# Two head groups to a tile in layer 0's attention, side work one step earlier in attentions 1 and 3, folding in other PSUM banks, and the last rows of two expert blocks in both halves of the array's rows

## The chip, the cores and the metric

The kernel runs on one core of a Trainium2 chip. The metric is the device time of one execution in microseconds. A core has five engines that work beside each other: TensorE (PE in the profile: matrix products into PSUM, with its weight loads shown as PEld), VectorE (DVE), ScalarE (ACT), GpSimd (POOL) and SyncE (SP, which here only issues transfers).

## What is computed

The reference is a network of four layers on x of shape (4, 256, 256), that is four batches of 256 tokens with 256 features, all in float32. Each layer adds an attention over a context (4, 512, 128) and then a feed-forward part:

```python
x = x + L0_xattn(layernorm(x), ctx, ...)   # 16 heads of 16; the last 16 context rows have a softmax of their own,
                                           # ctx @ Wo + bo with both results added
x = x + L0_ffn(layernorm(x), ...)          # 64 arrows of rank 16, the 4 longest of each token
x = x + L1_xattn(layernorm(x), ctx, ...)   # 16 heads of 128 on 8 key/value heads
x = x + L1_ffn(layernorm(x), ...)          # 8 experts of 176, 2 of each token, and a shared expert of 352
x = x + L2_xattn(...);  x = x + L2_ffn(...)  # two experts of 512, one of each token
x = x + L3_xattn(...);  x = x + L3_ffn(...)  # the 64 strongest tokens of each batch through 256-1024-256
```

An expert of layer 1 computes `silu(x @ wg.T) * (x @ wu.T) @ wd.T`. Its 176 inner features are 128 + 48, so its down product is one matmul with 128 contraction rows and one with 48.

## The kernel before

**Order.** The body stands in `tc.manual_schedule`, with the engines PE, ACT, DVE and POOL in the order in which the program is written: each engine takes its instructions strictly in that order, so where a call stands decides what waits behind what. Loads are issued on SP's queue. The stages are, in microseconds of the profiled span: layer 0's attention 0 to 153, its FFN with the folding of layer 1's weights to 243, attention 1 to 576, layer 1's FFN with folding of layer 2 to 702, attention 2 to 1035, layer 2's FFN with folding of layer 3 to 1091, attention 3 to 1436, and the last FFN.

**PSUM.** Up to the end of layer 0's FFN, `bank` (L850) hands out a ring of six banks for all tags but "o", which has two. Later there are four banks "s", two "mm", one "t" and one "o". A tile in a bank waits until the previous tile in it has been read.

**Layer 0's attention.** The loop at L1585 goes over batches b and four head groups hg of four heads, each in two steps (kp), so that a batch has steps i = 0 to 7. A step computes the scores of four heads (L1321: heads of 16 rows in the four 32-row groups of the array), their exponentials on ACT (L1325), and the products with the values of the step before (L1331, L1340). The value tile has 32 columns for a head: 16 columns of ones, which give the sums, and 16 of values. So a head group's result has 128 rows, half of which are sums. `quotient` (L1348) transposes within blocks of 32, takes reciprocals, transposes back and multiplies, all on DVE; POOL adds the two softmaxes into `oT[:, hg]` (L1360). `output0` (L1362) multiplies the four head groups' tiles with `wo0`, whose rows for the sums' places are zero, in four accumulating matmuls for each chunk of 128 tokens. `output_bias` (L1278) does it once for the bias. `ahead` works for the next batch: projections, and at i = 2 to 4 the norm of keys and queries, whose last step is the product at L1231 on DVE into `pad`; that is transposed at L1296 at the head of steps 6 and 7. `between` calls `output0(b - 1)` at i = 4 and 5:

```python
            if b > 0 and i in (4, 5):
                output0(b - 1, (i - 4,))
```

**Layer 0's FFN** goes over eight chunks with class `Arrows` (L1384); `turned` (L1435) transposes what POOL made in `twof` (L1427), `output` makes the result.

**Folding.** `folding` (L974) joins query and key weights into `m_sb` (L985 on PE, L993 on ACT) and value and output weights into `n_sb` (L1001 on PE, L1004 on DVE), eight times two heads for a layer, as a generator whose steps the stages take in between their own work.

**Layer 1's FFN.** `chosen` and `turned1` make the routing as side work of attention 1: `beside1` (L2117) is called at each unit hp of a batch. The pairs of token and expert are sorted into 23 blocks of 128 slots (NBLK), each of one expert, whose number is read into a register. A block gathers its tokens, transposes them (`turn_in`, L2303, one bank "t"), copies its expert's gate and up weights (`weights`, L2317 on DVE), makes gate and up (`rise`, L2325), silu on ACT and product on DVE, and then in `fall` the down products (L2341 with 128 rows, L2344 with 48), scaled by ACT (L2348) and stored by SP. The loop keeps three blocks going:

```python
                    blocks[j + 2].weights()
                    blocks[j + 2].turn_in()
                if 0 <= j + 1 < NBLK:
                    blocks[j + 1].rise()
                if 0 <= j < NBLK:
                    blocks[j].fall()
```

**Layers 2 and 3.** `Block2.turn_in` (L2605) does the same for layer 2's blocks. `beside3` (L3051) has the last layer's routing (class `Router`) as side work of attention 3.

Of the kernel before, what the change touches and what calls it, by code (L numbers as in the profile page):

```python
# [9 lines left out]
F32 = mybir.dt.float32  # L10
# [3 lines left out]
ALU = mybir.AluOpType  # L14
# [821 lines left out]
def bounded_path(ctx: ExitStack, tc: tile.TileContext, t, out: bass.AP, over):  # L836
# [137 lines left out]
    def folding(L, m_sb, n_sb):  # L974

        for i in range(4):
# [4 lines left out]
            for g in range(2):  # L981
# [18 lines left out]
                pn = bank("mm", [P, 2, D], f"pn_{L}_{i}_{g}")  # L1000
# [25 lines left out]
    with tc.manual_schedule(engines={E.PE, E.Activation, E.DVE, E.Pool}):  # L1026
# [42 lines left out]
        wo0 = l0.tile([P, 4, D], F32, tag="wo0", name="wo0")  # L1069
        nc.sync.dma_start(wo0, t["L0_wo"].rearrange("(g p) n -> p g n", p=P))  # L1070
# [34 lines left out]
        vals = [l0.tile([P, NK, H0, 32], F32, tag=f"vals{i}", name=f"vals{i}") for i in range(2)]  # L1105
        vals_d = [l0.tile([P, H0, 32], F32, tag=f"vals_d{i}", name=f"vals_d{i}") for i in range(2)]

        def ones_of_values():
# [9 lines left out]
            for i in range(2):  # L1118
                nc.gpsimd.memset(vals[i][:, : NK - 1, :, :HD0], 1.0)
                nc.gpsimd.tensor_copy(  # L1120
                    vals[i][:, NK - 1, :, :HD0], rows[:, 0:1, None].to_broadcast([P, H0, HD0])
                )
                nc.gpsimd.tensor_copy(vals_d[i][:, :, :HD0], rows[:, 1:2, None].to_broadcast([P, H0, HD0]))
# [61 lines left out]
        def project_v(b):  # L1185

            wv = by_head(wkv, 2 * HD0)[:, :, :, HD0:]
            for k0 in range(0, NK + 1, 2):
                pv = bank("mm", [P, 2, H0, HD0], f"pv{b}_{k0}")
                for k in range(k0, min(k0 + 2, NK + 1)):  # L1190
                    ck = c_last[:, b % 2, k - NK + 1, :] if k >= NK - 1 else cT[:, b, k * P : (k + 1) * P]
                    nc.tensor.matmul(pv[:, k - k0], lhsT=ck, rhs=wv[:, int(k == NK)], start=True, stop=True)
                if k0 < NK:
                    nc.scalar.copy(vals[b % 2][:, k0 : k0 + 2, :, HD0:], pv)
                else:
                    nc.scalar.copy(vals_d[b % 2][:, :, HD0:], pv[:, 0])
# [67 lines left out]
        bcol = l0.tile([P, 4, P], F32, tag="bcol", name="bcol")  # L1264

        def bias_rows():

            nc.vector.tensor_tensor(brow[:, 0, :], brow[:, 0, :], brow[:, 1, :], ALU.add)

        def bias_columns():  # L1270
            pc = bank("o", [P, 4], "pbrow")
            for g in range(4):
                nc.tensor.matmul(
                    pc[:, g : g + 1], lhsT=brow[:, 0, g * P : (g + 1) * P], rhs=ident[:1, :1], start=True, stop=True
                )
            nc.vector.tensor_copy(bcol, pc[:, :, None].to_broadcast([P, 4, P]))

        def output_bias():  # L1278
            pb = bank("mm", [P, D], "pbo")
            for g in range(4):  # L1280
# [1915 lines left out]
```

## Time and profile before

| what | value |
|---|---|
| median of 3 runs | 1453.56 us (1453.41 to 1455.87) |
| profiled execution, its own time | 1455.58 us |
| its span, first to last instruction | 1453.9 us |
| granted TensorE clock, mean | 0.994 |
| TensorE busy | 1421.4 us, 98% |
| DVE, ACT, POOL busy | 63%, 40%, 47% |
| output0's matmuls (L1366) | 64 records, mean 390 ns |
| down product, 128 rows and 48 rows (L2341, L2344) | 46 records each, mean 383 and 428 ns |

Times in the profile are microseconds from the span's start. A row of a timeline has the start, the duration, the engine, the line, the operation, the tile written and the tiles read, the shape and the number of records. Square brackets name how long the engine had been idle and the instruction that ended it. A float32 matmul leaves two records.

### The profile page before, as it was taken

The numbers are of one execution on the slowest core, as the hardware profiler recorded it, in microseconds if no ns is written. First come the engines' busy times: TensorE is split into PE (matmuls) and PEld (weight loads), VectorE is DVE, ScalarE is ACT, GpSimd is POOL, SyncE is SP. The second block draws the span as 40 slices with busy tenths as digits, with TensorE's granted clock in tenths as the row PEclk, the third lists the DMA queues.
The fourth block names the chain that finished last, engine by engine and source line by source line (L and its number), as shares of the span: only waits on it lengthen the run. The fifth ranks groups of instructions, "written<-read, shape, count | busy, mean of one in ns | idle before, by whom it ended". The sixth has DMA issues, their size and how long they took to land.

```text
span 1453.9 us, 20222 instructions
## 1 busy us (share of the span) xinstructions
PE 1421.4 (98%) x7421; PEld 937.0 (64%) x7421; DVE 914.0 (63%) x2004; ACT 585.9 (40%) x1124; POOL 677.1 (47%) x796
## 2 busy tenths in 40 slices
PE   9999999999999999999999999999999999999998
PEld 7665676566556666777556666655875566666656
DVE  6666773666676556543576666548755766767675
ACT  4666343433433332244543333333454433333331
POOL 2222232576655454131366665665314765456560
PEclk9999999999999999999999999999999999999999
DMA  5000220310000001164020000000331000000000
GB/s 167 2 2 2 73 72 1 79 32 0 8 1 8 1 8 32 39 203 103 30 72 2 23 1 1 8 0 8 95 124 44 19 1 1 0 1 0 0 1 32
DMA packets 49591, 47.06 MB, mean 32 GB/s; under 512 B 8169, under 2 KB 45386, under 8 KB 49484
## 3 DMA queue, kind: packets, MB, share of 16 engines
q1 hardware_dynamic: 45884, 37.56, 8.6%
q0 software_dynamic: 2496, 6.82, 1.8%
q8 instruction: 61, 1.00, 0.3%
q10 hardware_dynamic: 1104, 1.31, 0.3%
q14 instruction: 46, 0.38, 0.1%
HBM read 38.86 MB, written 6.82 MB: 31 GB/s over the span
## 4 chain that ended last, share of the span: by engine, by line
PE 88%; DVE 7%; POOL 2%; issue 1%; ACT 1%; DVEq 0%; ACTq 0%; POOLq 0%
PE ps L1817 22%; PE po L1825 21%; PE paq L1787 5%; PE pao L1787 4%; PE pbq L1787 4%; PE pbo L1787 4%; PE pgu L2325 2%; PE ps L1321 2%; PE pyf L1448 2%; PE po L1331 2%; PE paf L1398 1%; PE py L1907 1%; PE pm L985 1%; PE psh L2161 1%; PE pn L1001 1%
## 5 line engine op out<-in xcount | busy, mean ns | idle before, releaser
L1836 POOL TENSOR_TENSOR half<-pT 128x1024 f32<-128x1024 f32 x93 | 218.8, 2353 | 322.6 <-ACT pT L1820 255.2
L1817 PE MATMUL ps<-qT,cT 128*128 128x512 f32 x768 | 345.5, 592 | 0.0
L1825 PE MATMUL po<-pT,c_sb 128*128 128x512 f32 x768 | 345.3, 592 | 0.0
L1820 ACT ACTIVATE pT<-ps,mbias 128x512 f32<-128x512 f32 x384 | 263.7, 687 | 155.5 <-PE ps L1817 143.9
L1825 PEld LDWEIGHTS po<-pT,c_sb 128*128 128x128 f32 x768 | 145.8, 190 | 183.2 <-issue 183.2
L1817 PEld LDWEIGHTS ps<-qT,cT 128*128 128x128 f32 x768 | 138.9, 190 | 138.4 <-issue 137.0
L1829 ACT COPY oT<-po 128x512 f32<-128x512 f32 x96 | 56.2, 586 | 265.0 <-PE po L1825 265.0
L1872 POOL TENSOR_TENSOR oT<-oT,wide 128x512 f32<-128x512 f32 x90 | 115.5, 1304 | 27.9 <-DVE wide L1871 27.9
L1325 ACT ACTIVATE pT<-ps 128x512 f32<-128x512 f32 x128 | 66.1, 603 | 37.8 <-PE ps L1321 37.6
L1797 DVE TENSOR_TENSOR qT<-qT,paq 128x128 f32<-128x128 f32 x90 | 25.5, 283 | 85.8 <-ACT qT L1796 85.7
L1797 DVE TENSOR_TENSOR w<-w,pao 128x128 f32<-128x128 f32 x21 | 6.0, 285 | 109.4 <-ACT w L1796 109.4
L1844 DVE TENSOR_TENSOR half<-half 128x512 f32<-128x512 f32 x96 | 71.0, 740 | 2.5 <-POOL half L1836 2.2
L1846 DVE STREAM_TRANSPOSE turned<-half 128x512 f32<-128x512 f32 x96 | 68.3, 712 | 6.3
L1787 PEld LDWEIGHTS paq<-xnT_a,m_sb 128*128 128x128 f32 x360 | 57.9, 191 | 21.5 <-issue 10.6
L1787 PE MATMUL paq<-xnT_a,m_sb 128*128 128x128 f32 x360 | 71.4, 280 | 0.1
L1787 PE MATMUL paq<-xx,m_x 128*128 128x128 f32 x360 | 69.8, 276 | 0.0
L1850 DVE TENSOR_REDUCE sums<-turned 128x16 f32<-128x512 f32 x96 | 65.9, 686 | 3.4
L1787 PE MATMUL pao<-n_x,ox 128*128 128x128 f32 x336 | 65.4, 276 | 0.3 <-POOL ox L1713 0.3
L1871 DVE STREAM_TRANSPOSE wide<-rz 128x512 f32<-128x512 f32 x96 | 62.2, 686 | 0.1
L1796 ACT COPY qT<-paq 128x128 f32<-128x128 f32 x90 | 23.9, 265 | 89.9 <-PE paq L1787 89.8
L1800 DVE TENSOR_TENSOR qT<-qT,pbq 128x384 f32<-128x384 f32 x90 | 49.9, 554 | 9.4
L1787 PEld LDWEIGHTS paq<-xx,m_x 128*128 128x128 f32 x360 | 54.6, 192 | 0.0
(445 smaller groups left out, 2612.9 us busy)
## 6 DMA issues: line engine op xcount, KB each, us to landing
wo<-in_L_wo SPq DMA_DIRECT2D x12, 512.0 KB
wq<-in_L_wqT SPq DMA_DIRECT2D x11, 512.0 KB
yd<-yr SPq DMA_DIRECT2D x23, 128.0 KB
w<-in_F_w SPq DMA_DIRECT2D x4, 512.0 KB
xd<-xn_f SPq DMA_DIRECT2D x7, 256.0 KB
wk<-in_L_wkT SPq DMA_DIRECT2D x11, 128.0 KB
wv<-in_L_wvT SPq DMA_DIRECT2D x11, 128.0 KB
x_sb<-in_x SPq DMA_DIRECT2D x4, 256.0 KB
```

The costliest lines, as they stand in the source:

```text
L1325: nc.scalar.activation(pT[kp][:, j], ps[j], AF.Exp)
L1787: nc.tensor.matmul(p[:, at, :], lhsT=lhsT, rhs=rhs, start=(k == 0 and at == 0), stop=(k == len(of) - 1 and i == which[-1]),)
L1817: nc.tensor.matmul(ps, lhsT=cT[:, b, k * P : (k + 1) * P], rhs=qT, start=True, stop=True)
L1820: nc.scalar.activation(pT[:, k, :], ps, AF.Exp, bias=mbias[:, b, k : k + 1])
L1825: nc.tensor.matmul(po, lhsT=c_sb[:, b, k, :], rhs=pT[:, k], start=(k == 0), stop=(k == NK - 1))
L1829: done["head"] = nc.scalar.copy(raw, po).ins
L1836: nc.gpsimd.tensor_tensor(half, pT[:, 0:2], pT[:, 2:4], ALU.add)
L1844: nc.vector.tensor_tensor(part, half[:, 0], half[:, 1], ALU.add)
L1846: nc.vector.transpose(turned.rearrange("p f i -> p (f i)"), part)
L1850: nc.vector.tensor_reduce(sums[b, hp // 4][:, hp % 4, :], turned, AX.X, ALU.add)
L1871: nc.vector.transpose(wide, rzs[b, hp // 4][:, hp % 4, :, None].to_broadcast([P, NB, 32]))
L1872: eng.tensor_tensor(outs[b, hp], outs[b, hp], wide.rearrange("p f i -> p (f i)"), ALU.mult)
```

## The change

1. **Heads of layer 0 packed.** The values of even head groups go to columns 16 to 31 of a head's 32, those of odd ones to columns 0 to 15, with the ones in the other half (`halves`). So an even and an odd group fill opposite halves of one tile of `oT`, into which POOL adds: `oT`, `wo0`, the bias rows and columns have 2 parts instead of 4. The value weights are sorted into `wvo` by four copies on POOL; the reciprocals are put into a tile whose other half is zero, so that the sums' places become zero. `wo0` is loaded in eight transfers of 32 KB in place of one of 512 KB. (The value tiles, the fills with ones and the bias rows are indexed to match; these lines are left out below.)
2. **Layer 0's order.** `output0(b - 1)` stands at i = 6 and 7 for b = 1 and 2; the first `Arrows`' turned and output stand before `output0(B - 1)`.
3. **Folding.** After layer 0 the tile `pn` is in the banks "o" and "t" by turns instead of "mm".
4. **Layer 1's blocks.** The transposes use the banks "t" and "o" by turns; the first two blocks' weights are copied earlier. The down products' 48 last rows are done for two blocks together, at the odd one: the even block's in rows 0 to 47, the odd block's in rows 64 to 111, for which a copy `wdx` of its weights is made by DVE. Both blocks' results are scaled and stored after that, from the banks "mm".
5. **Side work.** `beside1` is one unit earlier. `beside3` too for the Router's making; its gathered and rest are one unit later.
6. **Layer 2.** `Block2.turn_in` uses "t" and "o" by turns.

```diff
...
-                pn = bank("mm", [P, 2, D], f"pn_{L}_{i}_{g}")
+                pn = bank("mm" if "ring" in banks else "ot"[g], [P, 2, D], f"pn_{L}_{i}_{g}")
...
-        wo0 = l0.tile([P, 4, D], F32, tag="wo0", name="wo0")
-        nc.sync.dma_start(wo0, t["L0_wo"].rearrange("(g p) n -> p g n", p=P))
+        wo0 = l0.tile([P, 2, D], F32, tag="wo0", name="wo0")
+        wo0r = t["L0_wo"].rearrange("(q o j i x) n -> o j i x q n", q=2, o=2, j=4, i=2)
+        for o in range(2):
+            for j in range(4):
+                r0 = 32 * j + HD0 * (1 - o)
+                nc.sync.dma_start(wo0[r0 : r0 + HD0], wo0r[o, j, 1])
...
+        halves = [(slice(HD0, 32), slice(0, HD0)), (slice(0, HD0), slice(HD0, 32))]
+        rz0 = [l0.tile([P, 2 * S // 32, 2], F32, tag=f"rzh{i}", name=f"rzh{i}") for i in range(2)]
+        wvo = l0.tile([P, 2, 2, H0 // 2, HD0], F32, tag="wvo", name="wvo")
...
-            wv = by_head(wkv, 2 * HD0)[:, :, :, HD0:]
...
-                pv = bank("mm", [P, 2, H0, HD0], f"pv{b}_{k0}")
+                pv = bank("mm", [P, 2, 2, H0 // 2, HD0], f"pv{b}_{k0}")
...
-                    nc.tensor.matmul(pv[:, k - k0], lhsT=ck, rhs=wv[:, int(k == NK)], start=True, stop=True)
-                if k0 < NK:
-                    nc.scalar.copy(vals[b % 2][:, k0 : k0 + 2, :, HD0:], pv)
-                else:
-                    nc.scalar.copy(vals_d[b % 2][:, :, HD0:], pv[:, 0])
+                    nc.tensor.matmul(pv[:, k - k0], lhsT=ck, rhs=wvo[:, int(k == NK)], start=True, stop=True)
+                for o, (h, _) in enumerate(halves):
+                    if k0 < NK:
+                        nc.scalar.copy(vals[b % 2][:, k0 : k0 + 2, o, :, h], pv[:, :, o])
+                    else:
+                        nc.scalar.copy(vals_d[b % 2][:, o, :, h], pv[:, 0, o])
...
-            for g in range(4):
-                nc.tensor.matmul(pb, lhsT=bcol[:, g, :], rhs=wo0[:, g, :], start=(g == 0), stop=(g == 3))
+            for g in range(2):
+                nc.tensor.matmul(pb, lhsT=bcol[:, g, :], rhs=wo0[:, g, :], start=(g == 0), stop=(g == 1))
...
-            rz = small.tile([P, NB0], F32, tag="rz0", name=f"rz0_{b}_{hg}")
-            nc.vector.reciprocal(rz, z[:, :, 0])
-            nc.vector.transpose(z, rz[:, :, None].to_broadcast([P, NB0, 32]))
+            odd = hg % 2
+            rz = rz0[odd]
+            nc.vector.reciprocal(rz[:, :, 1 - odd], z[:, :, HD0 * odd])
+            nc.vector.transpose(
+                z.rearrange("p f (i x) -> p f i x", i=2), rz[:, :, :, None].to_broadcast([P, NB0, 2, HD0])
+            )
...
-            nc.gpsimd.tensor_tensor(oT[:, hg, :], o[:, 0], o[:, 1], ALU.add)
+            oT = oT[:, hg // 2, :]
+            nc.gpsimd.tensor_tensor(oT, oT if odd else o[:, 1], o[:, 0], ALU.add)
+            if odd:
+                nc.gpsimd.tensor_tensor(oT, oT, o[:, 1], ALU.add)
...
-                for hg in range(4):
+                for q in range(2):
...
-                        lhsT=oTs[b][:, hg, c * P : (c + 1) * P],
-                        rhs=wo0[:, hg, :],
-                        start=(hg == 0),
-                        stop=(hg == 3),
+                        lhsT=oTs[b][:, q, c * P : (c + 1) * P],
+                        rhs=wo0[:, q, :],
+                        start=(q == 0),
+                        stop=(q == 1),
...
+        for n in range(2):
+            wv = by_head(wkv, 2 * HD0)[:, n, :, HD0:].rearrange("p (q o j) x -> p o q j x", q=2, o=2)
+            for o in range(2):
+                nc.gpsimd.tensor_copy(wvo[:, n, o].rearrange("p (q j) x -> p q j x", q=2), wv[:, o])
...
-            if b > 0 and i in (4, 5):
-                output0(b - 1, (i - 4,))
+            i0 = 4 if b == B - 1 else 6
+            if b > 0 and i in (i0, i0 + 1):
+                output0(b - 1, (i - i0,))
...
-            oTs[b] = w0.tile([P, 4, S], F32, tag="oT0", name=f"oT0_{b}")
+            oTs[b] = w0.tile([P, 2, S], F32, tag="oT0", name=f"oT0_{b}")
...
+        arrows[0].turned()
+        arrows[0].output()
...
-            arrows[n].turned()
+            if n:
+                arrows[n].turned()
...
-                arrows[n].output()
+                if n:
+                    arrows[n].output()
...
-            if hp == 4:
+            if hp == 3:
...
-            elif hp == 5:
+            elif hp == 4:
...
-            elif hp == 6:
+            elif hp == 5:
...
-            elif hp == 7:
+            elif hp == 6:
...
-                    pt = bank("t", [P, ND, P], f"pxg{self.j}")
+                    pt = bank("to"[self.j % 2], [P, ND, P], f"pxg{self.j}")
...
+                    self.rows = slice(64 * (j % 2), 64 * (j % 2) + FL)
+                def other_rows(self):
+                    self.wd = fp.tile([P, D], F32, tag="wdx", name=f"wdx{self.j}", bufs=1)
+                    nc.vector.tensor_copy(self.wd[self.rows, None, :], wd2[:FL, bass.ds(self.e, 1), :])
...
-                    self.gT = fp.tile([P, 2, P], F32, tag="gT", name=f"gT{j}")
-                    nc.vector.tensor_tensor(self.gT[:, 0, :], sg[:, 0, :], pp[:, 1, :], ALU.mult)
+                    self.gT = fp.tile([P, P], F32, tag="gT", name=f"gT{j}")
+                    if j % 2 == 0:
+                        state["gR"] = fp.tile([P, P], F32, tag="gR", name=f"gR{j}")
+                    self.gR = state["gR"]
+                    nc.vector.tensor_tensor(self.gT, sg[:, 0, :], pp[:, 1, :], ALU.mult)
...
-                        self.gT[:FL, 1, :], sg[64 : 64 + FL, 1, :], pp[64 : 64 + FL, 2, :], ALU.mult
+                        self.gR[self.rows], sg[64 : 64 + FL, 1, :], pp[64 : 64 + FL, 2, :], ALU.mult
...
-                    j = self.j
-                    py = bank("o", [P, D], f"pyr{j}")
-                    nc.tensor.matmul(
-                        py, lhsT=self.gT[:, 0, :], rhs=wd1[:, bass.ds(self.e, 1), :], start=True, stop=False
-                    )
+                    self.py = bank("mm", [P, D], f"pyr{self.j}")
...
-                        py, lhsT=self.gT[:FL, 1, :], rhs=wd2[:FL, bass.ds(self.e, 1), :], start=False, stop=True
+                        self.py, lhsT=self.gT, rhs=wd1[:, bass.ds(self.e, 1), :], start=True, stop=False
...
+                def last_rows(self):
+                    rhs = self.wd[self.rows] if self.j % 2 else wd2[:FL, bass.ds(self.e, 1), :]
+                    nc.tensor.matmul(self.py, lhsT=self.gR[self.rows], rhs=rhs, start=False, stop=True)
+                def store(self):
+                    j = self.j
...
-                    done["slots"] = nc.scalar.activation(yr, py, AF.Copy, scale=state["wslot"][:, j : j + 1]).ins
+                    done["slots"] = nc.scalar.activation(
+                        yr, self.py, AF.Copy, scale=state["wslot"][:, j : j + 1]
+                    ).ins
...
+            blocks[0].weights()
...
+            blocks[1].weights()
...
-                    blocks[j + 2].weights()
+                    if j >= 0:
+                        blocks[j + 2].weights()
...
+                    if j % 2 == 0 and j + 1 < NBLK:
+                        blocks[j + 1].other_rows()
+                    if j % 2 or j == NBLK - 1:
+                        pair = blocks[j - j % 2 : j + 1]
+                        for one in pair:
+                            one.last_rows()
+                        for one in pair:
+                            one.store()
...
-            pt = bank("t", [P, ND, P], f"pxg2_{self.j}")
+            pt = bank("to"[self.j % 2], [P, ND, P], f"pxg2_{self.j}")
...
-            if hp == 4:
+            if hp == 3:
...
-            elif hp == 5:
+            elif hp == 4:
...
-            elif hp == 6:
+            elif hp == 5:
...
-            elif hp == 7:
+            elif hp == 6:
...
-            if hp == 0:
+            if hp == 1:
...
-            elif hp == 1:
+            elif hp == 2:
...
-            elif hp == 2 and b == 3:
-                picked(0)
+                if b == 3:
+                    picked(0)
```

## The prediction

> **What bounds the kernel now.** I read the profile from coarse to fine: first the page's busy shares and the chain that ended last, then the waits of TensorE, then the timeline around each place that the change touches.
>
> ```profile
> PE 1421.4 (98%) x7421; PEld 937.0 (64%) x7421; DVE 914.0 (63%) x2004; ACT 585.9 (40%) x1124; POOL 677.1 (47%) x796
> ...
> PE 88%; DVE 7%; POOL 2%; issue 1%; ACT 1%; DVEq 0%; ACTq 0%; POOLq 0%
> ```
>
> TensorE is busy 1421.4 of 1453.9 us, so almost every matmul that goes shortens the span, unless something else is late there. What all its waits hold together is the other 32 us. The waits that the change touches are these (who waits, for whom; us in total, times, longest):
>
> ```profile
> PE pxg L2608 <- ACT xnT_f L940: 1.7, 1, 1.7
> PE py L1366 <- POOL oT L1360: 1.6, 1, 1.6
> ...
> PE pT L1296 <- DVE y_sb L1374: 1.4, 1, 1.4
> PE pn L1001 <- ACT m_sb L993: 1.4, 2, 0.7
> ...
> PE pgu L2325 <- DVE we L2317: 0.7, 1, 0.7
> ...
> PE pysh L2178 <- ACT m_sb L993: 0.6, 1, 0.6
> ...
> PE pm L985 <- DVE n_sb L1004: 0.5, 1, 0.5
> ...
> PE pxg L2306 <- ACT xgT L2308: 0.5, 1, 0.5
> ```
>
> The timeline of TensorE (start, duration, records; an f32 matmul leaves two records) gives the price of the matmuls. In layer 0:
>
> ```profile
> 78.00 1.99 PE L1366 MATMUL py<-wo,oT 128*128 128x256 f32 x8
> 79.92 1.15 PE L1321 MATMUL ps<-qT,kT 16*128 16x256 f32 x16
> 81.00 0.66 PE L1296 MATMUL pT<-ident,pad 128*128 128x128 f32 x4
> 83.07 1.09 PE L1296 MATMUL pT<-ident,pad 128*128 128x128 f32 x8 [1.42 <-DVE y_sb L1374]
> ```
>
> From start to start, one chunk of the output projection (four matmuls) takes 79.92 - 78.00 = 1.92 us, or 0.48 each. The next row is the evidence on row groups: eight matmuls of 16 rows, in four row groups, take 1.08 us, although each, alone, would need about what a matmul of 256 columns needs (0.43 to 0.48). In layer 1's block loop:
>
> ```profile
> 632.30 0.44 PE L2306 MATMUL pxg<-ident,xg 128*128 128x128 f32 x2
> 632.57 1.49 PE L2325 MATMUL pgu<-xgT,we 128*128 128x128 f32 x12
> 633.90 0.60 PE L2341 MATMUL pyr<-wd,gT 128*128 x2
> 634.43 0.70 PE L2344 MATMUL pyr<-wd,gT 48*128 x2
> ```
>
> No wait stands in these rows and the period is 2.76 us (629.54 to 632.30), so TensorE bounds the loop. ACT works 1.39 us and DVE 1.12 us per block.
>
> [...] 8 x 0.43 / 1.08 = 3.2 times at L1321, and the 48-row product at L2344 costs no less than the 128-row one at L2341. Two halves of 64 rows are shown by no row here. [...] L2341 shows at most 0.10 (633.90 to 634.43 is 0.53, against 0.43 of streaming). [...]
>
> **Layer 0, heads packed two groups to a tile.** The value projection's even and odd head groups go to opposite 16-row halves of the 32-row blocks, so that output0 needs 2 matmuls for each chunk instead of 4: 16 matmuls x 0.48 = 7.7 us. output_bias loses 2 of 4 (-0.9 or so), but all of its saving in batch 0 falls before a wait (1.13 us at 47.21, in truth the pad product of DVE that ends there), so only 0.24 remains. Total work gone: about 8.5 us. What is added: each copy of projected values is split (L1194: 583 ns for 512 elements; two of 256 cost about 0.38 each by the 0.38 us of L1196), +0.5 us ACT per batch, in the open only before the first values (+0.45, at 32). Eight more POOL adds at 740 ns, four copies of the packed value weights and the fills are hidden: POOL is idle 64.7 us waiting for DVE at L1360, and works here some 0.74 of a 4.3 us step. If that cover were gone, 8 x 0.74 = 5.9 us. On SP's queue, one 512 KB load becomes eight of 32 KB, ahead of bo0 and the FFN's weights: 7 more issues at 0.48 us are +3.4 us for what is behind them, which first serves at output_bias (40.50; the queue was at 10.1) and later. Hidden, and fewer bytes; uncovered it would be 3.4.
>
> output0(b-1) moves in batches 1 and 2 from steps 4, 5 to 6, 7. Batch 1: the 1.42 wait above goes (transposes queued behind an evacuation that stands behind the quotient on DVE). But with both chunks gone from its front, TensorE now reaches the first transpose near 77.0, while DVE ends the pad product there near 78.3 (power on ACT to 75.25, then 0.25 + 0.72 + 0.26 + 1.76): a new wait of 1.3. Behind it, in TensorE's order, stand the values, then the moved chunk and the scores, whose fourth bank waits for DVE's half of the query (0.4). Sum: -1.92 - 1.42 + 1.3 + 0.4, about -1.6; I take -1.4. Batch 2 had no wait there (115.62 follows at once) and gets the same one: -1.92 + 1.3, rounded to -0.8. Batch 3, not moved: -1.92. At the end arrows[0].turned and output go ahead of output0(3), so the 1.58 wait for POOL's oT goes, but the turning needs POOL's twof (ends 162.14), which costs about 1.9 of wait: -1.92 - 1.58 + 1.9, or -1.6 to -2.0; -1.8. **Layer 0: +0.45 - 0.24 - 1.4 - 0.8 - 1.9 - 1.8 = -5.7 us.** Bounds -2 (DVE and ACT take it all back in batches 1 and 2 and at the end) and -11.
>
> **Folding.** pn goes to the banks o and t by turns in layers 1 and 2. In layer 1's fold the stretch 681.73 to 701.88 is 20.15 us against some 17.0 of matmuls: the waits are 0.63 (pysh), 0.69 (pn), 0.49 (pm) and smaller ones. One, behind an ACT table load of 1.28 us at 682.33, stays in part; -2.0 (bounds 0 and -3). In layer 2's fold the stretch 1079.0 to 1091.4 has 12.44 against 10.94, so there is 1.5 to gain; but bank t is also wanted by the transposes of attention 3's first norm, and DVE's copies of pn (687 ns each) stand behind that norm in DVE's order: copy at about 1088.3, against 1087.3 wanted, and again for the router's product. I take +1.6 (bounds -1 and +2.5).
>
> **Layer 1's blocks.** Before the loop the alternating banks and two earlier weight copies remove 0.46 (613.19) and 0.74 (614.37): -1.2. In the loop the two 48-row products of a pair run in rows 0 to 47 and 64 to 111: 0.43 goes per pair, and half of the 0.10 around the dynamic address of the second: 0.48 x 11 pairs = -5.3. If they do not overlap, -0.5; at best, with all gaps halved, -6.5. Added: 11 copies of 48x256 on DVE (by L2317, 547 ns for 736 elements, at most 0.4 each), hidden under the 1.4 us that DVE has spare in a block; uncovered 4.4. The stores now stand together at the pair's end: two at 474 ns, free at 0.55 and 1.0 us after the last rows, while TensorE first does the next transposes and 1.33 of gate and up, and wants the bank at 1.6.
>
> **The rest.** Attention 1's and 3's side work one step earlier: units there have no stall except two of 0.32 at 1260.87 and 1344.63; -0.1 and -0.6, so -0.7 (bounds +0.5, -1). Layer 2's turn_in by turns: the 1.66 at 1048.71 and 0.46 at 1026.29 go: -2.1.
>
> **Sum.** -5.7 - 2.0 + 1.6 - 1.2 - 5.3 - 0.7 - 2.1 = -15.4 us. The profiled execution took 1455.58, 2.0 above the median of 1453.56, with 1.7 us outside its span of 1453.9; I carry the difference over: 1440.2 for a profiled run like it, **1438.2** against the median.
>
> **Rivals.** (B) Less arrives: DVE's pad product and ACT's exponentials take back more of layer 0 (-2 instead of -5.7), and the two halves do not overlap (-0.5 instead of -5.3): 1438.2 + 3.7 + 4.8 = 1446.7. For it: 2.06 us of exponentials for each 4.3 us step, a chain that nothing shortens; against it: the four-fold overlap at L1321. (C) More goes: no new wait in layer 0 (8.5 of work and 3.0 of waits, less 1.3: -10.2), no loss in layer 2's fold: 1438.2 - 4.5 - 1.6 = 1432.1. (D) Slower: each pair's last rows wait for the copy of the odd block's weights, which sits in DVE's queue behind the next block's copy and products. One such round is 1.12 + 0.4 = 1.5 us; if it were bare, and the overlap worthless, 11 x 1.5 = +16.5 against -10.1 from the rest: 1460. It decides from 0.92 us per pair on. DVE's spare 1.4 us per block speaks against it. (E) That packing does not do what it says: nothing hints at it in layer 0, where the instruction count falls by itself; for the halves it lies in B.
>
> **How the numbers follow.** A measurement of this kernel tells apart about 0.2% (2.9 us). Forecast 0.50 (its own range 1434.5 to 1442.5), B 0.22, C 0.18, D 0.06, and 0.04 for gains cancelled to within 2.9 us. Faster 0.90, same 0.04, slower 0.06. Leaving out D, the cancelled case and the far part of B and C, the range is 1431.5 to 1447.
>
> **What would show it.** L1366's successor with 32 records and chunks of 0.96; no wait for y_sb before the transposes, but one of 1 to 1.5 for the pad product, in batches 1 and 2; a pair period near 5.0 with the two 48-row products starting together; no pxg wait in layers 1 and 2; in layer 2's fold a wait of attention 3's transposes for DVE's n_sb. I am wrong if the pair stays near 5.5, or if layer 0 ends less than 4 or more than 8 us earlier.

## The result, and the profile after

The changed kernel takes 1434.0 us in the median of 4 runs (1433.48 to 1437.53), against 1453.63 us for the kernel before beside it: ratio 0.9867, with a 95% interval of 0.9848 to 0.9885. The profiled execution took 1433.84 us with a span of 1432.1. So 19.6 us went in the medians and 21.8 in the two spans; 15.4 were forecast. The median lies in the range that the prediction stated (1431.5 to 1447), and half a microsecond under the narrower one that it gave for its main forecast (1434.5 to 1442.5).

The page's busy shares, of the kernel after:

```profile
PE 1403.2 (98%) x7381; PEld 927.0 (65%) x7381; DVE 899.5 (63%) x2016; ACT 586.3 (41%) x1136; POOL 683.8 (48%) x816
```

TensorE still bounds the kernel: 18.2 us of its busy time are gone and 3.6 us of its idle time. Its waits in the kernel after (who waits, for whom; us in total, times, longest):

```profile
PE puTf L1461 <- POOL twof L1453: 3.0, 2, 1.8
PE pxn_a L937 <- DVE n_sb L1004: 2.9, 2, 2.0
PE pT L1315 <- DVE pad L1244: 2.7, 3, 1.5
...
PE pgu L2367 <- ACT xgT L2344: 1.3, 3, 0.8
...
PE pwr L3142 <- DVE n_sb L1004: 0.8, 1, 0.8
...
PE pz L1893 <- DVE sums L1886: 0.3, 1, 0.3
```

The waits for y_sb and oT in layer 0 are gone, and those for the pad product and for twof stand in their place, as forecast. New ones for n_sb stand before attention 3, also as forecast. The wait for pz (a product with the sums of the softmax, in attentions 1 to 3) has almost gone, and that was in no step of the forecast. It was the longest entry of the kernel before:

```profile
PE pz L1857 <- DVE sums L1850: 3.4, 3, 2.6
```

Aligning the two timelines by the tiles that TensorE writes gives this account (start of a matmul after, less its start before). "Layer 2's fold" is the folding of layer 2's weights during layer 1's FFN, which the prediction calls layer 1's fold, and so on:

| stretch of the span (before) | forecast | in the two traces |
|---|---|---|
| layer 0 with its FFN, to 243.9 | -5.7 | -3.8 |
| attention 1 and layer 1's start, to 606.0 | -0.1 | -3.2 |
| start of the blocks, to 614.4 | -1.2 | -1.5 |
| the blocks, to 677.5 | -5.3 | -6.8 |
| layer 2's fold, to 701.9 | -2.0 | -2.1 |
| attention 2, to 1026.3 | 0 | -1.7 |
| layer 2's blocks, to 1079.0 | -2.1 | -1.7 |
| layer 3's fold, to 1091.9 | +1.6 | +1.8 |
| attention 3 and the end | -0.6 | -2.6 |

Two things of TensorE's clock are in these differences without being part of the change. First, the full clock begins at 5.84 us in the profiled execution before and at 7.53 in the one after: until then a record of TensorE's warm-up takes 0.21 us from start to start, from then on 0.11. That puts the kernel after 0.8 us behind at 10 us, and the lag lasts through layer 0. The other profiled executions begin between 5.86 and 7.74, so a comparison of two traces from the start of the span is good to about 0.9 us. Second, there are windows in which the clock is at one half (565.63 to 569.04 us before, 48.48 to 51.90 after, and others); experiment 3 comes to them.

Layer 0 in batch 1 after the change (timeline of TensorE):

```profile
79.41 1.50 PE L1315 MATMUL pT<-ident,pad 128*128 128x128 f32 x12 [0.59 <-DVE pad L1244]
80.85 1.07 PE L1350 MATMUL po<-pT,vals 128*32 128x256 f32 x16
81.85 1.13 PE L1392 MATMUL py<-wo,oT 128*128 128x256 f32 x4
82.91 0.71 PE L1340 MATMUL ps<-qT,kT 16*128 16x256 f32 x6
84.12 1.13 PE L1340 MATMUL ps<-qT,kT 16*128 16x256 f32 x10 [0.51 <-DVE qT L1327]
```

All three parts of that step's working are there: a chunk of output0 takes 82.91 - 81.85 = 1.06 us with two matmuls, the transposes wait for the pad product (0.59; I had 1.3), and the scores' last bank waits for DVE's half of the query (0.51; I had 0.4).

Layer 1's block loop after, an odd block:

```profile
630.07 0.60 PE L2385 MATMUL pyr<-wd,gT 128*128 x2
630.59 0.48 PE L2391 MATMUL pyr<-wd,gR 48*128 x1
630.60 0.48 PE L2391 MATMUL pyr<-wdx,gR 48*128 48x256 f32 x1
630.91 0.38 PE L2391 MATMUL pyr<-wd,gR 48*128 x1
630.92 0.38 PE L2391 MATMUL pyr<-wdx,gR 48*128 48x256 f32 x1
631.23 0.44 PE L2342 MATMUL pxg<-ident,xg 128*128 128x128 f32 x2
631.50 1.49 PE L2367 MATMUL pgu<-xgT,we 128*128 128x128 f32 x12
632.83 0.60 PE L2385 MATMUL pyr<-wd,gT 128*128 x2
633.26 0.38 PE L2342 MATMUL pxg<-ident,xg 128*128 128x128 f32 x2
```

The even and the odd block's 48-row products start 10 ns apart, record by record: the halves do overlap. Pairs follow at 4.75 us (the transposes after each pair start at 626.48 and 631.23) instead of 5.52: 0.77 each, where I had 0.48.

Before attention 3 the forecast loss has come:

```profile
1064.40 1.02 PE L1001 MATMUL pn<-wo,wv 128*128 128x512 f32 x2
1067.44 0.66 PE L937 MATMUL pxn_a<-ident,xn_a 128*128 128x128 f32 x4 [2.02 <-DVE n_sb L1004]
```

### The profile page after: what moved, and what is told of

Read it like the earlier page. It is cut to its first block, busy times and chain, and to the rows that moved or that the text cites. A ratio compares the mean times of both kernels' runs of the same rounds, so it can differ in the third digit from the quotient of the medians.

```text
span 1432.1 us, 20213 instructions
## 1 busy us (share of the span) xinstructions
PE 1403.2 (98%) x7381; PEld 927.0 (65%) x7381; DVE 899.5 (63%) x2016; ACT 586.3 (41%) x1136; POOL 683.8 (48%) x816
```

## The experiments

Every group was run beside the kernel before, on one chip; between groups the median of before differs (1455.2, 1455.4, 1454.1 and 1453.5 us). Times are therefore compared by their ratio to before, and the parts by the traces.

**1. The pairing alone, on the kernel before.**

```diff
+                    if j % 2 or j == NBLK - 1:
+                        pair = blocks[j - j % 2 : j + 1]
+                        for one in pair:
+                            one.last_rows()
+                        for one in pair:
+                            one.store()
```

(with last_rows, other_rows and the banks "mm" as in the change; nothing else of it)

> The kernel before with only the pairing of layer 1's last rows (products, copy of the odd block's weights, stores at the pair's end). Theory 1 (the pair stands by itself: a pair's period goes from 5.52 to about 4.75 us, as in the trace after): 11 x 0.77 = 8.5 us off, less some 1 us of new waits at the stores: about 1446. Theory 2 (only the overlap of 0.43 and half a step is the pair's; the rest of the gain in the loop comes from the alternating banks and earlier weights): 11 x 0.48, about 1448.5.

Measured: 1449.1 us (1448.29 to 1449.51) against 1455.2, ratio 0.9959 (0.9944 to 0.9974), so 3.8 to 8.1 us off. Both theories' times lie in that interval. The trace decides: from 618.50 (before) to 673.70 the start of the same matmul moves by 6.9 us, 0.77 for each of nine pairs; one more pair, near the end, gains nothing, because a wait of 0.57 us falls in it (ACT's scaled copy waits for an earlier store to land). Theory 1 holds for the loop: the 0.77 needs neither the alternating banks nor the earlier weights.

**2. The pair's products in the same rows.**

```diff
-                    self.rows = slice(64 * (j % 2), 64 * (j % 2) + FL)
+                    self.rows = slice(0, FL)
```

(the odd block gets its own tile of last rows, and no copy of its weights)

> The changed kernel, but the odd block's last rows lie in the same array rows 0 to 47 as the even block's, without the copy of its weights; grouping, banks and stores stay. Theory 1 (the two products overlap because they lie in different halves): a pair's period rises from 4.75 to about 5.2, 11 x 0.43 = +4.7 us: about 1438.7. Theory 2 (the gain is from grouping the four products, fewer switches and register steps, and the halves do nothing): 4.75 stays, 1434 or less.

Measured: 1438.71 us, ratio 0.9892 (0.9877 to 0.9908). The timeline of TensorE in this run:

```profile
621.57 1.13 PE L2391 MATMUL pyr<-wd,gR 48*128 x4
622.63 0.44 PE L2342 MATMUL pxg<-ident,xg 128*128 128x128 f32 x2
```

The four records now take 1.06 us in place of 0.64, and the period of a pair rises by 0.43, in every pair. So of the 0.77 the overlap gives 0.43, and grouping (each even block's first product is followed at 0.43 by the next block's transposes, without the 0.10 step and the gap after L2344) gives 0.34. The loop as a whole ends only 2.3 us later than in the kernel after, because waits for a store's buffer (experiment 9) disappear at the slower pace.

**3. The packing alone.** The kernel before with the head groups packed, output0 and Arrows left where they were:

```diff
-                for hg in range(4):
+                for q in range(2):
                     nc.tensor.matmul(
```

> The kernel before with only layer 0's packing of two head groups into a tile, output0 left at steps 4 and 5 and the order at the end as before. Theory 1 (TensorE bounds layer 0, so the removed matmuls count): 4 x 1.92 less 0.45 at the start, 0.24 of the bias, and 0.74 of POOL's second add at the end, about -6.5: 1447. Theory 2 (DVE's quotient and ACT's exponentials take most of it back without the moves): -2 to -3, about 1451.

Measured: 1456.21 us (20 runs), ratio 1.0014 (1.0007 to 1.0021): a trifle slower than before, though 8.5 us of matmuls are gone. Both theories missed. The waits of TensorE:

```profile
PE pT L1315 <- DVE y_sb L1400: 3.6, 2, 2.3
PE pz L1887 <- DVE sums L1880: 3.4, 3, 2.6
PE py L1392 <- POOL oT L1386: 3.3, 1, 3.3
```

and the timeline in batch 1:

```profile
80.28 1.39 PE L1315 MATMUL pT<-ident,pad 128*128 128x128 f32 x8
83.93 0.66 PE L1315 MATMUL pT<-ident,pad 128*128 128x128 f32 x4 [2.26 <-DVE y_sb L1400]
84.51 1.31 PE L1350 MATMUL po<-pT,vals 128*32 128x256 f32 x16
85.75 2.09 PE L1340 MATMUL ps<-qT,kT 16*128 16x256 f32 x16
87.77 2.82 PE L1315 MATMUL pT<-ident,pad 128*128 128x128 f32 x12
```

TensorE has fewer matmuls ahead of the transposes, but DVE's y_sb, which frees their bank behind quotient and norm, ends no earlier (at 83.9, before at 83.0), so the wait grows from 1.42 to 2.26; likewise POOL's oT at the end from 1.58 to 3.31 us. And after the wait everything on TensorE is slow: sixteen score records take 2.02 us start to start instead of 1.08. The view of stretches (its columns: stretch, length, busy time and count of PE, PEld, DVE, ACT, POOL, then the granted TensorE clock, DMA share, GB/s) shows why:

```profile
85.00:92.00 7.00, 7.00 (x56) 4.53 (x52) 2.93 (x9) 3.13 (x6) 0.02 (x1) 0.52 0.00 0
166.00:171.00 5.00, 5.00 (x17) 3.83 (x18) 4.83 (x8) 1.17 (x2) 1.24 (x1) 0.66 0.00 0
```

The clock was granted at one half. The trace's record of the clock has whole windows of 3.41 us at half: four of them in layer 0 and its FFN here, none there in the kernel before. At half the clock TensorE gets through 1.7 us less work in each (an estimate, half of 3.41), together 6.8. Layer 0 with its FFN ends 3.5 us later than before. Taking the 6.8 off would put it 3.3 earlier; that is a subtraction and not a run, and experiment 11 shows that not all of a window's cost comes back when the window goes.

The mean clock of every execution is on record, and it bears this out beyond the profiled one. Of the twenty executions, ten had a mean clock of 0.992 and took 1454.8 to 1455.6 us; the other ten had 0.989 or 0.990 and took 1456.8 to 1459.8. A window lowers the mean by 0.0012 (half of 3.41 in 1454 us), so two more of them, 3.4 us, would make the difference.

**4. The moves alone,** on the kernel before (output0 at steps 6 and 7, the first Arrows ahead of the last output0):

```diff
+            i0 = 4 if b == B - 1 else 6
+            if b > 0 and i in (i0, i0 + 1):
+                output0(b - 1, (i - i0,))
```

> The kernel before with only the order of layer 0 changed: output0 of batches 0 and 1 at steps 6 and 7, the first Arrows' turned and output before the last output0; four matmuls for each chunk as before. Theory 1 (packing and moves pay only together): the moves alone take the 1.42 for y_sb and the 1.58 for oT and bring waits of 0.6 twice for the pad product and 1.8 for twof: within 1.5 us of before. Theory 2 (the moves alone make most of layer 0's gain, the removed matmuls little): -3 to -4.

Measured: 1455.52 us, ratio 1.0005 (0.9996 to 1.0013). Theory 1: the moves alone give nothing. In the trace y_sb and oT are waited for no more, while twof takes 3.0 us (1.3 before) and the pad product 1.2. Layer 0 with its FFN ends 1.8 us later, which is one window at half clock (132.5 to 135.9) that the kernel before did not have; the trace of experiment 1, whose layer 0 is that of the kernel before, has it too, so it isn't the moves'. So packing alone and moves alone brought no time as measured, and together they took 3.8 us off layer 0 in the traces.

**5. output0 back at steps 4 and 5,** in the changed kernel:

```diff
-            i0 = 4 if b == B - 1 else 6
-            if b > 0 and i in (i0, i0 + 1):
-                output0(b - 1, (i - i0,))
+            if b > 0 and i in (4, 5):
+                output0(b - 1, (i - 4,))
```

> The changed kernel with output0(b-1) at steps 4 and 5 in all batches, as before the change. Theory 1 (packing pays only with this move: with half the matmuls ahead of the transposes, TensorE merely waits longer for DVE's late y_sb): the waits for y_sb return with 2.3 and 1.3 us against 0.59 + 0.59 + 0.5, and idle stretches of this length can bring a window of half clock (1.7 us each): +2 to +5, about 1437. Theory 2 (the move is worth only the 1.42 us it was predicted to trade for the pad product's wait): within 1 us of 1434.

Measured: 1439.76 us, ratio 0.9895 (0.9878 to 0.9912) against the change's 0.9856 to 0.9867. The waits for y_sb are back (3.5 us, the longest 2.2), and at once the half clock, two windows long, at 84 to 91 us. Layer 0's attention ends 3.7 us later than in the kernel after, 4.5 with the difference of 0.8 at the start of the clock. Theory 1; but 3.4 of it is the two windows, and the waits themselves are the smaller part.

**6. The first Arrows after the last output0 again,** in the changed kernel:

```diff
-        arrows[0].turned()
-        arrows[0].output()
         output0(B - 1)
```

> The changed kernel with the first Arrows' turned and output again after output0 of the last batch. Theory 1 (POOL's second add per odd head group makes oT later: the wait at the last output0 grows from 1.58 to about 3.3 us, as in the packing alone, while the 1.76 for twof goes): +1.5, about 1435.5, more if the wait brings a window of half clock. Theory 2 (the prediction: one wait for the other, nothing gained): 1434.

Measured: 1436.45 us, ratio 0.9872 (0.9857 to 0.9887), too close to the change to tell by time. In the trace the wait for oT is 3.3 us. The FFN of layer 0 goes on 1.0 us later than in the kernel after; but this execution was 0.6 us ahead when layer 0's attention ended, because its full clock began at 6.23 us instead of 7.53. So the order is worth 1.6 us there, and 1.5 at the end of layer 0: Theory 1. The prediction had put 1.9 paid for twof against 1.58 saved, and missed that POOL's second add lengthens the 1.58.

**7. Attention 1's side work one unit later again,** in the changed kernel:

```diff
-            if hp == 3:
+            if hp == 4:
                 ahead1[b] = Norm(b - 1, f"f1_{b - 1}")
```

(and so for the three steps after it)

> The changed kernel with attention 1's side work one unit later again. Theory 1 (the last batch's routing chain of DVE at the last unit delays the sums of the softmax: a wait of 2.6 us for pz at the end of attention 1, less 0.8 us of waits for oT that then go): +1.9, and +1.7 where a half-clock window follows: 1436 to 1437.5. Theory 2 (the prediction: -0.1 for this part; the wait in the trace before was due to something else): 1434.

Measured: 1436.0 us, ratio 0.988 (0.9861 to 0.9899). Its waits of TensorE:

```profile
PE pz L1893 <- DVE sums L1886: 2.9, 2, 2.6
```

The 2.6 us are back. In the kernel before, the timeline shows the mechanism: the routing of the last batch stands between po's last matmul and the sums.

```profile
558.61 0.17 DVE L2088 TENSOR_REDUCE mx<-pl 128x2 f32<-128x16 f32 x1 [4.49 <-PE pl L2072]
...
561.79 0.68 DVE L1842 TENSOR_TENSOR half<-pT 128x512 f32<-128x512 f32 x1
...
564.05 0.69 DVE L1850 TENSOR_REDUCE sums<-turned 128x16 f32<-128x512 f32 x1
564.88 0.41 PE L1857 MATMUL pz<-sums,quad 128*128 128x64 f32 x2 [2.64 <-DVE sums L1850]
```

From 558.61 to 561.79 DVE is in `chosen`, which had waited for TensorE; only then does it reach the last unit's sums, and TensorE, at 562.2 out of work, waits for them until 564.88. One unit earlier, `chosen` is over by 552.3 and the sums are ready. Theory 1 is right on the wait, but not on its sum: the 0.8 us of waits for oT did not go, and over attention 1 the trace is 2.9 us longer than in the kernel after, where +1.9 was expected.

In the kernel before, a window at half clock comes right behind this wait; here none does, although the wait is as long. The view of stretches, in the kernel before:

```profile
562.22:565.63 3.41, 0.77 (x8) 0.78 (x8) 2.61 (x6) 0.27 (x1) 0.00 (x0) 1.00 0.01 2
565.63:569.04 3.41, 3.41 (x19) 3.41 (x18) 3.34 (x5) 0.00 (x0) 1.27 (x1) 0.50 0.00 0
```

and here:

```profile
556.08:559.49 3.41, 1.97 (x18) 1.77 (x16) 3.06 (x15) 0.27 (x1) 0.00 (x0) 1.00 0.00 0
559.50:562.91 3.41, 2.22 (x20) 2.25 (x21) 2.71 (x6) 0.00 (x0) 0.13 (x1) 1.00 0.00 0
562.91:566.30 3.39, 2.92 (x17) 2.17 (x15) 3.32 (x5) 0.00 (x0) 2.14 (x2) 1.00 0.00 0
```

The trace's record of the clock gives this window 3.413 us, and in three traces the windows lie a whole number of 3.413 us apart: in the kernel before they begin at 565.63, 599.76 and 777.25 us, 10 and 52 times that, in the kernel after at 48.48 and 591.20, 159 times, and in experiment 3 at 47.67, 85.21 and 167.13, 11 and 24 times. Before, the wait fell whole into one such stretch, and TensorE was busy for 0.77 us of it; here it was divided between two. So the window at 565.63 goes with the wait that the change removed, but it does not come in every execution. In the traces of experiments 1, 3 and 4 the same wait leaves TensorE idle for 2.1, 1.9 and 1.9 us of one such stretch; a window follows in the first two and none in the third.

**8. Attention 3's side work as before,** in the changed kernel:

```diff
-            if hp == 1:
+            if hp == 0:
                 routers[b - 2].gathered()
```

(and so for the other steps)

> The changed kernel with attention 3's side work as before. Theory 1 (trace after against before: 0.9 us in each of two batches and 0.6 at the last pz): +2.4, about 1436.4. Theory 2 (the prediction: only the two waits of 0.32 go): +0.6, about 1434.6.

Measured: 1436.52 us, ratio 0.9873 (0.9857 to 0.9888). In the trace, attention 3 runs 2.6 us longer than in the kernel after, where the forecast had 0.6: Theory 1. The parts can be read off: 0.9 in each of two batches around the gathered tokens (of which 0.32 is the wait that the prediction names), and 0.7 at the last pz, before which the routing's DVE work stood as in attention 1.

**9. Repairs: layer 3's folding and the stores.** Layer 3's pn goes back to "mm", the scaled results have four buffers, and the copy of the odd block's weights lies in unused rows of their own tile, which makes room:

```diff
-                pn = bank("mm" if "ring" in banks else "ot"[g], [P, 2, D], f"pn_{L}_{i}_{g}")
+                pn = bank("mm" if "ring" in banks or L == 3 else "ot"[g], [P, 2, D], f"pn_{L}_{i}_{g}")
-                    self.wd = fp.tile([P, D], F32, tag="wdx", name=f"wdx{self.j}", bufs=1)
+                    self.wd = wd2[:, (self.j // 2) % 2, :]
-                    yr = fp.tile([P, D], F32, tag="yr", name=f"yr{j}", bufs=3)
+                    yr = fp.tile([P, D], F32, tag="yr", name=f"yr{j}", bufs=4)
```

> The changed kernel with layer 3's folding back in the banks mm, four buffers instead of three for the scaled results of layer 1's blocks, and the copy of the odd block's weights in unused rows of the weights' own tile. Theory 1 (bank t held by the folding costs 2.02 + 0.78 us of waits before attention 3, of which the folding in mm gives back about 1.6 net; the third-last store's landing costs about 1.3 us of waits in the block loop): about -2.9, 1431. Theory 2 (what waits in layer 3's folding waits for ACT or DVE all the same): within 1 us of 1434.

Measured: 1432.28 us (1431.07 to 1434.09), ratio 0.9844 (0.9831 to 0.9858). By the ratios that is 1.7 to 3.3 us less than the changed kernel, with intervals that overlap, so the traces have to show it. In the trace the blocks end 1.6 us earlier than in the kernel after (waits of 0.84 and 0.20 for ACT's copies, which stood behind a scaled result without a free buffer, are gone), and attention 3 begins 1.5 us earlier relative to the blocks of layer 2, in spite of a wait of 0.7 that comes there instead. Theory 1; the profiled execution lost part of it to a half-clock window in attention 2.

**10. The changed kernel again.**

> The changed kernel itself, beside the same runs of the kernel before as the two that follow. 1434 where before takes 1453.6, and up to 2 us more where windows of half clock fall in it: 1434 to 1437.

Measured: 1433.73 us, ratio 0.9856 (0.9841 to 0.9871).

**11. Added matmuls that keep TensorE active.** In all profiled executions so far, one to three windows are at half clock around layer 1's list of slots (`plist`, sixteen matmuls of 46 columns that find the token of every slot; two in the kernel after, 591.20 to 598.03 us), and in all kernels with the packing there is one at the first transposes of layer 0's loop (48.48 to 51.90 in the kernel after). This kernel is that of experiment 9 with matmuls on the identity that nobody reads:

```diff
+                    for _ in range(5 if n == 0 else 1):
+                        nc.tensor.matmul(pw[:, : P if n == 0 else 64], lhsT=ident, rhs=ident[:, : P if n == 0 else 64], start=True, stop=True)
                     nc.tensor.matmul(
                         state["plist"], lhsT=at
...
                 elif i == 6:
+                    if b == 0:
+                        warm(6)
                     transposed(n, range(3))
```

> The changed kernel with layer 3's folding in the banks mm, four buffers for the scaled results, and added matmuls on the identity that nobody reads: six before batch 1's first transposes, five before the first matmul of the list of slots and a half one before each further. Theory 1 (the windows of half clock at 48 us and 590 to 597 come from TensorE's low activity there, and cost 1.5 and about 3.4 us): they go, and the time falls from best1's 1432.3 to about 1428. Theory 2 (the windows come whatever TensorE does, or the added matmuls cost what they save): 1432 or more.

Measured: 1430.45 us, ratio 0.9836 (0.9822 to 0.9849). That is between the theories. But for the last 4 us, the windows are gone from the whole span, and the mean clock of all five executions is 0.997 to 0.999, where in experiment 9 it was 0.993 or 0.994. Little of it became time. The list takes 6.9 us, where with half clock it took 5.6. In layer 0, TensorE now waits 1.14 us for DVE's qT at the next transposes, a wait that the slower matmuls had covered, and the layer ends only 0.3 us earlier than in experiment 9.

**12. Fewer of them, and none that takes a bank.** In the list before every second matmul, in layer 0 into the bank that the transposes then fill:

```diff
-                    for _ in range(5 if n == 0 else 1):
+                    for _ in range(5 if n == 0 else n % 2):
...
+                if b == 1 and c == 0:
+                    for _ in range(6):
+                        nc.tensor.matmul(pt[:, 0, :], lhsT=ident, rhs=ident, start=True, stop=True)
```

> As the kernel before this one (layer 3's folding in mm, four buffers, added matmuls on the identity), but the six added matmuls of layer 0 go into the bank that the transposes then overwrite, so that no bank of the ring is taken away, and in the list of slots a half one stands before every second matmul only. Theory 1 (the added matmuls cost 1.1 us by the bank and 0.2 us each in the list, and half of them hold the clock): 1.1 + 1.6 less, about 1428. Theory 2 (with half of them TensorE's activity is too low and the windows of half clock return at the list): 1430.5 or more.

Measured: 1427.96 us (1427.32 to 1428.38), ratio 0.9821 (0.9808 to 0.9834); the mean clock is 0.999 in all five executions. The time is Theory 1's, but only one of its two terms came. Seven fewer half matmuls take 1.6 us off the list, as expected: from its first matmul to the next product's it is 5.35 us, in experiment 11 it was 6.91. The 1.1 us "by the bank" stayed: the wait for DVE's qT is 1.18 us, in experiment 11 it was 1.14, so the bank was not its cause. In its place 0.9 of the 2.5 us between the two traces come from the first 8 us, where the full clock began at 5.86 instead of 7.74 us; that part is luck of the profiled execution. The two executions of experiment 11 that also had a mean clock of 0.999 took 1429.5 and 1429.8 us, 1.5 to 1.9 us above this median.

The same two stretches (columns as above), in the kernel after:

```profile
47.00:51.00 4.00, 3.23 (x24) 2.35 (x28) 3.83 (x9) 2.60 (x5) 0.77 (x2) 0.69 0.00 0
...
590.00:597.00 7.00, 6.99 (x32) 6.33 (x32) 3.94 (x20) 0.00 (x0) 0.93 (x1) 0.59 0.00 0
```

and in this kernel:

```profile
47.00:51.00 4.00, 3.47 (x45) 2.29 (x44) 3.79 (x10) 2.29 (x5) 1.48 (x3) 1.00 0.00 0
...
590.00:597.00 7.00, 7.00 (x49) 6.44 (x49) 4.01 (x18) 0.00 (x0) 2.04 (x2) 1.00 0.05 13
```

In the second stretch it gets through 49 records, ten of them of added matmuls, instead of 32. From before the list to the start of the blocks it takes 1.8 us less than experiment 9. This kernel beats the changed one by 5 to 6 us, the repairs of experiment 9 included.

## Why the prediction was right or wrong, point by point

**Layer 0** (-5.7, measured -3.8): the mechanism was right in both directions, and the waits that it forecast came (0.59 twice where I had 1.3, 0.51 where I had 0.4, 1.76 where I had 1.9). The sum was mis-sized. The sign "I am wrong if layer 0 ends less than 4 us earlier" was met, by 0.2 us; five other profiled executions with the same layer 0 (experiments 2 and 7 to 10) have 3.8 to 4.3. Taking out what the start of the clock adds in each, all six have 4.5 to 4.6.

| part of layer 0 | forecast | in the two traces |
|---|---|---|
| the start and batch 0, to 60 us before | +0.2 | +1.3 |
| batch 1 | -1.4 | -1.3 |
| batch 2 | -0.8 | -1.2 |
| batch 3 | -1.9 | -1.2 |
| the end, with the FFN | -1.8 | -1.4 |

Of the first line, 0.8 is the start of the clock. About 0.3 is the window at half clock that follows the wait of 1.48 at 47.77; I had priced a wait at its own length and this window at nothing. Experiment 11 shows that it costs 0.3 there and not 1.7, since DVE's qT would have been waited for anyway. In batch 3 I counted the removed matmuls alone; a chunk takes 1.06 us instead of 0.96, and a wait of 0.23 for the FFN's normalized tokens appears. The rest of that line is open. Two roundings in the working cancel: batch 1's sum is -1.64 and was taken as -1.4, batch 2's is -0.62 and was taken as -0.8.

Costing the packing and the moves as separate parts was also wrong in kind: experiments 3 and 4 show each of them at nothing. I had priced the move as 1.42 saved against 1.3 paid, but without it the packing brings a wait of 2.26 and a clock at one half. At the end, experiment 6 gives 1.5 for the order of the Arrows, where the working has a loss of 0.3.

**Folding** (-2.0 and +1.6): right, at -2.1 and +1.8, the second by the very transposes and copies that the step named. Experiment 9 confirms it by taking 1.5 of it back.

**The blocks** (-1.2 and -5.3): the start came at -1.5. The pair's term was undersized: 0.43 of overlap, an estimate from the row groups of L1321, was exact (experiment 2), but for the gaps I had 0.05 and they gave 0.34. The gap behind every L2344 (0.63 from its start to the next transposes, against 0.43 of streaming), which stood in the rows that I showed, disappears for the even block altogether. From the 8.5 us that 11 pairs make, waits for stores take 1.6 back, in two of the pairs. I had taken the store's buffer for free after 1 us by counting only PSUM banks; the result tile has three buffers, and a store takes 5.5 us to land in the median, so in these two pairs the second store found none.

**The rest** (-0.7): wrong. "Units there have no stall except two of 0.32" overlooked the 2.64 us at the last pz of attention 1, the longest entry in the list of waits, because I read it as belonging to what comes after it and didn't ask what DVE was doing before its sums. Priced at -0.1, the earlier side work is worth -2.9 (experiment 7). In the two traces attention 1 gives -3.2: the wait with its slow restart is 2.9 of it and the window at half clock behind it 1.5, and 1.0 is lost to waits for oT, which that window had covered. Attention 3 gave -2.6, partly for the same reason (experiment 8).

**Attention 2** (0, measured -1.7): no part of the change; the profiled execution before had a half-clock window at 777 us that the one after lacks. The traces of experiments 1 and 9 have one at the same place, those of experiments 3 and 4, with the same code there, have none.

**The rivals.** B needed halves that don't overlap and a layer 0 that gives little; the first is refuted, the second half true for the packing by itself. C's total, 1432.1, lies nearest the result, but for other reasons than it gave: layer 0 did have its new waits, and layer 3's fold did lose. D's bare copy is nowhere to be seen. The stores that I had cleared cost something, though far from D's 0.92 us per pair. The forecast's direction and range held; its centre was 4.2 us high. The side work of attention 1 (2.8 beyond what I had given), that of attention 3 (2.0) and the blocks (1.5) make 6.3, and layer 0 takes 1.9 back. That this comes so near to 4.2 is partly luck, since it mixes parts of single traces, in which a window of half clock is 1.7 by half its length, with medians.

## What to carry to other kernels

Matmuls taken off a stretch need not pay until what the next matmul waits for is also moved; the packing and the reordering, which brought nothing each as measured, took 3.8 us off layer 0 together. Go through the list of the bound engine's waits from the top and say for every entry which part of the change touches it: the longest one here was settled by a part that I had priced at 0.1. Where a cheaper version makes the bound engine wait, look at its clock afterwards, and test what a half-clock window costs by taking it away: some matmuls on nothing were worth 1.8 us at the list of slots and 0.3 us in layer 0, where another wait took the window's place. And before two traces are compared, compare where their full clock begins: here that is worth up to 0.9 us, and it decides the reading of experiments 6 and 12.

## What the runs showed of the hardware that I had not expected

TensorE's clock falls to one half for windows of 3.41 us, singly (565.63 to 569.04 in the kernel before) or two in a row (591.20 to 598.03 in the kernel after), in the middle of a kernel in which TensorE is 98% busy. In the three traces compared in experiment 7 the windows lie on one grid of 3.413 us, and the same wait of 2.6 us brought one in the kernel before and none in experiment 7, where it was divided between two stretches. Ahead of the window at 565.63 TensorE was busy for 0.77 of 3.41 us, but ahead of that at 777.25 for 2.22, and of that at 48.48 in the kernel after for 1.93. What stood there was a wait of 2.64 us in the kernel before, of 2.26 in experiment 3 and of 2.25 in experiment 5, or one of 1.48 at 47.77 in the kernel after, or, from 596.35 to 599.76 in the kernel before, the list's matmuls of 46 columns with TensorE shown busy for 3.37 of 3.41 us. Yet two stretches with 1.97 and 2.22 us busy in experiment 7 brought none; what counts as activity, the traces do not show.

The windows also go with the spread of one kernel's times: in experiment 3 the ten executions with the lower mean clock are all slower than the ten others, and in experiment 12, at 0.999 in all of them, five executions lie within 1.1 us. That matmuls on the identity remove the windows was shown (experiments 11 and 12): from 10.2 us at half clock in the kernel after, before the end of its span, to none before the last 4 us.
